# Constant matmuls in TensorE's waits, stores on two queues, and contiguous transposes in the tail of an attention and Fourier kernel

## The chip, the cores and the metric

The kernel runs on one core of a Trainium2 chip. The metric is device time in microseconds (us). Four timed executions of the kernel before took 3204.36 to 3206.36 us, with a median of 3204.9 us. One execution was recorded by the hardware profiler; the page and the trace that are quoted here come from it.

Engines are named as the profile names them: PE is TensorE's matrix multiply and PEld its weight load, DVE is VectorE, ACT is ScalarE, POOL is GpSimd, SP is SyncE (here only a queue that issues DMAs). L12 is line 12 of the kernel file. A 32-bit float (f32) matmul leaves two records in the trace, and so does its weight load.

## The reference

The input is x, 4 images of 64 channels and 96 x 96 pixels, in f32. Two layers follow each other, each of the form x + layer(group_norm(x)):

```python
# layer 0: attention over the 9216 pixels, with sigmoid weights
energy = jnp.einsum('bcn,bcm->bnm', Q, K)          # Q, K: 8 channels
out = jnp.einsum('bcm,bnm->bcn', V, jax.nn.sigmoid(energy)).reshape(B, C, H, W) + x
scale = jax.nn.sigmoid(mlp(out.mean((2, 3))) + mlp(out.max((2, 3))))
y = out * scale[:, :, None, None]

# layer 1: a spectral convolution
u_hat = jnp.fft.rfft2(u, norm='ortho')
top = jnp.einsum('bchw,cohw->bohw', u_hat[:, :, :16, :16], R_pos)
bot = jnp.einsum('bchw,cohw->bohw', u_hat[:, :, H - 16:, :16], R_neg)
# all other modes are zero
y = jnp.fft.irfft2(v_hat, s=(H, W), norm='ortho')
```

Group norm has 32 groups of two channels. Only 32 rows (the first 16 and the last 16) times 16 columns of the spectrum are used, so layer 1 is four small products with constant matrices (along w, along h, back along h, back along w) with one channel mixing per mode between them.

## The kernel before

The four images are handled as two pairs; a pair's 2 x 64 channels fill the 128 partitions. Attention of pair 0 and then of pair 1 takes the first 3106 us. Layer 1 of pair 0 is done in small steps beside the attention of pair 1 (class `Hidden`, lines 223 to 334). Layer 1 of pair 1 has nothing left to hide behind: it is the tail, written out in program order from line 577 on, and it is what the change edits.

The tail, by its parts:

- **Statistics and the transform along w** (lines 618 to 631). For each of 12 strips of 8 image rows, DVE forms layer 0's result (`combine`, L158) and transposes the strip in blocks of 32 x 32 (L623); ACT sums the squares (L624); PE multiplies the transposed strip with the matrix `fw` (L631) into a two-bank tile `pa`. Four strips fill one `pa`.
- **The transform along h** (lines 636 to 645). After each fourth strip (n = 0, 1, 2) DVE transposes `pa` into a tile `a` (L637), and four matmuls add its part to the two banks `pu` (L642). They read `a` in consecutive elements as the moving operand. These matmuls stand in PE's order where the scheduler puts them: those of n = 1 stand ahead of the last strips' L631.
- **Statistics' end** (L655 to L660). The variance, `group_stats`' second and third step (matmul L136, DVE L138, POOL L139), and `spread` (matmuls L169), which turns them into a scale per channel.
- **The spectrum `u`** (L667 to L677). DVE transposes `pu` (L670), and ACT and DVE scale it into `ut` (L672 to L675, and L183).
- **Mixing** (`mix`, L185 to L209, called from L687). For each q from 0 to 7 and two halves: 8 matmuls (L198), then a copy from PSUM to a tile `vm` (L112 on DVE, L114 on ACT, in turns). There are four `vm` tiles. After the second half, four stores of 64 KB each write `vm` to a DRAM tensor `vd`; all 32 stores are issued by SP (L209).
- **The way back through DRAM** (L210 to L221). The mixed modes are read back in another order into `vt`, in 64 KB loads: four after q = 3, issued by POOL, and four after q = 7, two by SP and two by ACT. The loads of the second group wait for all stores of q = 4 to 7.
- **Back along h** (L693 to L704). 16 matmuls (L700) into 8 PSUM banks `pz`. Their moving operand is `vt`, viewed as `"q (k o) -> q o k"`: 16 elements that lie 64 elements apart, 16 times.
- **The transposes to `z`** (L705 to L710). Eight DVE transposes L708 read a bank in order and write `z[:H, :, ...]` with a step of 128 elements between consecutive elements.
- **Back along w and the result** (L713 to L727). For each of 8 groups, 12 matmuls (L720) whose weights are `z[rows, h, :]`, 128 consecutive elements, and whose moving operand is the constant `gw`; DVE adds the residual (L722), and after each second group three stores of 384 KB go out on SP and ACT (L726).

The mixing weights are 32 rows of 512 KB. Those that aren't there yet are loaded by POOL during the tail (L650, L590), each as soon as the tile that it takes the place of is free.

PSUM pools: `ps_m` (two buffers of one tag) serves the small matmuls of the statistics, `ps_v` (8 buffers) the mixing.

Of the kernel before, what the change touches and what calls it, by code (L numbers as in the profile page):

```python
# [40 lines left out]
P = 128  # L41
# [36 lines left out]
def tile_kernel(ctx: ExitStack, tc: tile.TileContext, x, cst, late, spec, out):  # L78
# [37 lines left out]
    def group_stats(stats, bank, name):  # L116
# [17 lines left out]
        def third():  # L134
            pv = bank(f"pv_{name}")
            nc.tensor.matmul(pv[:, 0:1], pav, t, start=True, stop=True)  # L136
            ve = small.tile([P, 1], F32, tag="ve", name=f"ve_{name}")
            nc.vector.tensor_scalar(ve, pv[:, 0:1], GN_EPS, None, ALU.add)  # L138
            nc.gpsimd.tensor_tensor(mr[:, 1:2], ve, nhalf, ALU.pow)  # L139

# [5 lines left out]
    class Layer1:  # L146


        def __init__(self, p, gate, bank, move, load_queue):
            self.p, self.gate, self.bank, self.move = p, gate, bank, move  # L150
            self.load_queue = load_queue
# [9 lines left out]
        def spread(self, mr):  # L161
# [5 lines left out]
            for b in range(2):  # L167
                for part in range(2):
                    nc.tensor.matmul(pr[bass.ts(part, C), bass.ts(b, 2)],  # L169
                                     ident[:, bass.ts(b, C)], mr, start=True, stop=True)  # L170
# [14 lines left out]
        def mix(self, q, half):  # L185
# [8 lines left out]
            for k in range(2):  # L194
                kw = half * 2 + k
                for g in range(4):
                    at = ((4 * q + g) * KW + SIDE * kw) * 4
                    nc.tensor.matmul(  # L198
# [9 lines left out]
            for g in range(4):  # L208
                nc.sync.dma_start(self.vd[4 * q + g], self.vms[q][32 * g:32 * g + 4 * SIDE, :])  # L209
            if q % 4 == 3:  # L210
                if self.vt is None:
                    self.vt = self.place_of_vt()
                row, M = 4 * SIDE * KW * C, KW // SIDE * C
                for b in range(2):
                    for slot in range(2):
                        to = 64 * b + 32 * slot + 4 * q - 12
                        of = self.vd[4 * q - 12, 2 * slot + b, :]
                        of = bass.AP(tensor=of.tensor, offset=of.offset,
                                     ap=[[row, 16], [4 * KW * C + M, SIDE], [1, M]])
                        self.load_queue(q, slot).dma_start(  # L220
                            self.vt[to:to + 16, :].rearrange("h (n m) -> h n m", n=SIDE), of)  # L221

    class Hidden(Layer1):


        def __init__(self, p, gate, bank, move, work):
            super().__init__(p, gate, bank, move, lambda q, slot: nc.sync)
# [349 lines left out]
    with tc.tile_pool(name="tail", bufs=1, reuse_waits="tile") as tail, \  # L577
# [22 lines left out]
        for i in range(4):  # L600
            wts[NSLOT - 4 + i] = w_mid[:, bass.ts(i, KW * C)]
            nc.gpsimd.dma_start(wts[NSLOT - 4 + i], spec[NSLOT - 4 + i])

        small_bank = psum("ps_m")
        l1 = Layer1(1, gate, lambda name: small_bank.tile([P, NB], F32, tag="m", name=name, bufs=2),
                    evacuate, lambda q, slot: nc.gpsimd if q == 3 else (nc.sync, nc.scalar)[slot])
# [10 lines left out]
        pu = [pu_bank.tile([P, NB], F32, tag=f"u{b}", name=f"pu_{b}") for b in range(2)]  # L617
        for s in range(NSTRIP):
# [11 lines left out]
            for k in range(NSQ):  # L630
                nc.tensor.matmul(pa[:, bass.ts(i, STRIP // NSQ)], fw[:, bass.ts(k, P)], v[:, k],  # L631
                                 start=(k == 0), stop=(k == NSQ - 1))
            if i < NSTRIP // NSQ - 1:
# [3 lines left out]
            nc.vector.transpose(a.rearrange("q (k c) -> q c k", c=SQ),  # L637
                                pa.rearrange("q (h c) -> q c h", c=SQ))
            for part in range(2):
                for b in range(2):  # L640
                    rows = bass.ts(b, C)
                    nc.tensor.matmul(pu[b], fh[rows, part, bass.ts(n, P)],  # L642
                                     a[rows, bass.ts(part, NB)],
                                     start=(n == 0 and part == 0),
                                     stop=(n == NSQ - 1 and part == 1))
# [9 lines left out]
        var = small.tile([P, 1], F32, tag="var", name="var")  # L655
        nc.vector.tensor_reduce(var, squares, AX.X, ALU.add)
        nc.vector.tensor_scalar(mv[:, 1:2], var, 1.0 / N, None, ALU.mult)
        for step in steps[1:]:
            step()
        l1.spread(mr)  # L660

# [22 lines left out]
        mix_bank = psum("ps_v", 8)  # L684
        l1.bank = lambda name: mix_bank.tile([P, NB], F32, tag="v", name=name)
        l1.place_of_vt = lambda: place_of("w0", "vt")
        for q in range(KH // 4):  # L687
            l1.mix(q, 0)
            l1.mix(q, 1)

# [5 lines left out]
        for i in range(4):  # L696
            for e in range(2):
                for b in range(2):
                    rows = bass.ts(b, 2 * KH)
                    nc.tensor.matmul(  # L700
# [4 lines left out]
        z = tail.tile([P, SQ, P], F32, tag="z", name="z_1")  # L705
# [107 lines left out]
```

## Time and profile before

| What | us |
|---|---|
| median of 4 timed executions | 3204.9 |
| their range | 3204.36 to 3206.36 |
| the profiled execution's own time | 3206.36 |
| its span, first to last instruction | 3204.6 |
| attention of both pairs, to the last L426 | 3106.5 |
| the tail, 3106.5 to 3204.6 | 98.1 |

The mean granted TensorE clock is 0.991 of full speed over the span. In the tail it is not: it goes between 1.0 and 0.5, as the stretches quoted in the prediction list.

How to read what is quoted: in a list of stretches each line is a stretch of the span, its length, then for PE, PEld, DVE, ACT and POOL the busy time and in brackets the number of instructions touching the stretch, then the granted clock, the mean busy share of the DMA engines and the GB/s that they moved. In a list of groups each line is a line of the kernel, engine and operation, output <- inputs, shapes, the count, and after the bar the busy time in us and the mean duration of one in ns. In the chain, each line is the start, the length and the instruction that the end of the program was waiting for in that stretch. An answer on one line of the kernel gives the count, and after it the shortest, the median and the longest duration in ns.

### The profile page before, as it was taken

The page shows a single profiled execution, that of the slowest core. Times are in us where ns is not written, and L with a number is a line of the kernel's source. Part 1 is how long each engine was busy: PE and PEld are TensorE (multiplying, and loading weights), DVE is VectorE, ACT ScalarE, POOL GpSimd, SP SyncE. Part 2 cuts the span into 40 slices and gives each one's busy share as a digit, 9 for nine tenths or more (in the row PEclk, how much of TensorE's full clock was granted, in tenths as well). Part 3 has the DMA queues.
Part 4 walks back from the last instruction along what each step waited for, and adds up shares of the span by engine and source line. Part 5 has one row for each costly group of instructions (what it writes and reads, how often), then busy time and mean ns, then how long its engine had stood idle before and what let it go on. Part 6 is the DMA issues. An engine that isn't in the chain of part 4 may idle for free.

```text
span 3204.6 us, 39104 instructions
## 1 busy us (share of the span) xinstructions
PE 3147.3 (98%) x17464; PEld 1068.4 (33%) x17464; DVE 399.8 (12%) x838; ACT 2432.8 (76%) x1765; POOL 22.4 (1%) x45
## 2 busy tenths in 40 slices
PE   7999999999999999999999999999999999999996
PEld 3333333333333333334333333333333333333334
DVE  4200000000000000003331110000000110000025
ACT  3688888888888888886677777777777777888871
POOL 0000000000000000000000000000000001000001
PEclk9999999999999999999999999999999999999997
DMA  3000000000000000000130100221010112000025
GB/s 139 1 1 1 1 1 1 1 1 1 1 1 1 1 1 1 1 1 1 40 92 14 40 1 30 82 70 37 13 28 10 40 36 97 33 1 1 11 77 177
DMA packets 39032, 86.78 MB, mean 27 GB/s; under 512 B 10672, under 2 KB 17584, under 8 KB 38768
## 3 DMA queue, kind: packets, MB, share of 16 engines
q1 hardware_dynamic: 32240, 61.75, 6.5%
q0 software_dynamic: 4880, 17.63, 1.5%
q10 hardware_dynamic: 1744, 4.91, 0.4%
q8 instruction: 136, 2.23, 0.3%
q14 instruction: 32, 0.26, 0.0%
HBM read 62.77 MB, written 21.50 MB: 26 GB/s over the span
## 4 chain that ended last, share of the span: by engine, by line
PE 97%; DVE 1%; DMA 1%; SPq 0%; issue 0%; ACT 0%; POOL 0%; ACTq 0%
PE acc L426 74%; PE e L415 18%; PE pv L385 1%; PE pv L198 1%; PE py L330 1%; PE pk L376 1%; PE pq L396 1%; DMA x<-in_x_dram 0%; PE py L720 0%; PE pt L253 0%; PE pz L309 0%; PE pa L631 0%; PE pu L290 0%; DVE z L708 0%; SPq L209 0%; PE pu L642 0%
## 5 line engine op out<-in xcount | busy, mean ns | idle before, releaser
L419 ACT ACTIVATE at<-e 128x1536 f32<-128x1536 f32 x1728 | 2412.5, 1448 | 683.4 <-PE e L415 683.2
L426 PE MATMUL acc<-at,vT 128*64 128x512 f32 x10368 | 2418.9, 601 | 0.0
L426 PEld LDWEIGHTS acc<-at,vT 128*64 128x64 f32 x10368 | 668.3, 136 | 1294.5 <-issue 1279.1
L415 PE MATMUL e<-q,kT 32*128 32x512 f32 x5184 | 636.4, 461 | 1.3 <-ACT at L419 1.3
L415 PEld LDWEIGHTS e<-q,kT 32*128 32x128 f32 x5184 | 257.9, 183 | 642.2 <-issue 583.0
L356 DVE TENSOR_SCALAR full_q<-pq,cs 128x256 f32<-128x256 f32 x36 | 17.4, 484 | 1557.2 <-PE pq L396 1557.1
L569 DVE SCALAR_TENSOR_TENSOR x<-acc,x 128x512 f32<-128x512 f32 x36 | 24.9, 691 | 294.3 <-PE acc L426 294.3
L385 PE MATMUL pv<-cs,x 128*128 128x128 f32 x288 | 43.4, 295 | 0.1
L332 DVE TENSOR_TENSOR x<-py,x 128x384 f32<-128x384 f32 x24 | 13.4, 558 | 226.0 <-PE py L330 226.0
L406 DVE CAST q<-q 32x256 fp32r<-32x256 f32 x144 | 40.9, 284 | 3.8
L385 PEld LDWEIGHTS pv<-cs,x 128*128 128x128 f32 x288 | 36.2, 197 | 14.2 <-DVE full_k L356 12.9
L505 DVE COPY ws<-pv 128x512 f32<-128x512 f32 x16 | 11.1, 691 | 216.3 <-PE pv L198 216.3
L364 DVE SCALAR_TENSOR_TENSOR q<-high_q,cs,full_q 64x256 fp32r<-64x256 f32 x72 | 34.6, 480 | 2.4
L505 DVE COPY xT<-pt 96x512 f32<-96x512 f32 x24 | 16.4, 685 | 114.1 <-PE pt L253 114.1
L356 DVE TENSOR_SCALAR full_k<-pk,cs 128x256 f32<-128x256 f32 x36 | 17.4, 483 | 103.4 <-PE pk L376 103.4
L387 DVE TENSOR_TENSOR vT<-pv,cs 128x512 f32<-128x512 f32 x36 | 24.9, 691 | 8.8 <-PE pv L385 8.8
L571 DVE TENSOR_REDUCE maxs<-x 128x1 f32<-128x512 f32 x36 | 24.7, 685 | 1.1
L376 PE MATMUL pk<-x,cs 128*64 128x256 f32 x144 | 23.3, 395 | 1.5 <-DVE x L144 1.5
L433 DVE BATCH_NORM_STATS2 stats<-x 128x6 f32<-128x512 f32 x36 | 22.2, 677 | 8.1 <-DMA x<-in_x_dram 8.1
L396 PE MATMUL pq<-x,cs 128*64 128x256 f32 x144 | 22.1, 386 | 0.0
L330 PE MATMUL py<-cs,ws 128*128 128x384 f32 x48 | 21.9, 539 | 0.0
L128 PE MATMUL pm_l<-mv_l,cs 128*128 128x1 f32 x8 | 1.7, 286 | 20.5 <-DVE mv_l L124 19.8
(96 smaller groups left out, 448.6 us busy)
## 6 DMA issues: line engine op xcount, KB each, us to landing
ws<-in_spec_dram SPq DMA_DIRECT2D x32, 512.0 KB
x<-in_x_dram SPq DMA_DIRECT2D x15, 512.0 KB
out_dram<-x SPq DMA_DIRECT2D x18, 384.0 KB
w<-in_spec_dram POOLq DMA_DIRECT2D x10, 512.0 KB, 6.6
old<-in_x_dram SPq DMA_DIRECT2D x12, 384.0 KB
x1d<-x SPq DMA_DIRECT2D x12, 384.0 KB
x<-x1d SPq DMA_DIRECT2D x12, 384.0 KB
w_early<-in_spec_dram POOLq DMA_DIRECT2D x9, 512.0 KB, 9.4
```

Source lines behind the costliest of these rows:

```text
L198: nc.tensor.matmul(pv[bass.ts(g, 32), :].rearrange("q (n k o) -> q n k o", n=SIDE, o=C)[:, :, k, :], self.ut[:, at:at + 32], self.wts[4 * ...
L330: nc.tensor.matmul(py[:, :4 * W], self.z[:, i, :], named("gw"), start=True, stop=True)
L356: nc.vector.tensor_scalar(u, src, bias, None, ALU.add)
L364: mark[0] = nc.vector.scalar_tensor_tensor(dst, h.bitcast(F32), is_low, u, ALU.mult, ALU.add)
L376: nc.tensor.matmul(pp[cols, :NB // 2], named("wk")[:, cols], src[:, e, :, :], start=True, stop=True)
L385: nc.tensor.matmul(pp[:, bass.ts(i, P)], xs[p][:, bass.ts(4 * s + i, P)], named("wv"), start=True, stop=True)
L396: nc.tensor.matmul(pq[rows, :half], named("wq")[:, rows], xs[p][:, n * NB + e * half:n * NB + (e + 1) * half], start=True, stop=True)
L406: nc.vector.tensor_copy(q[to:to + 32, cols], q[of:of + 32, cols])
L415: nc.tensor.matmul(eb[i // PART][:, i % PART, :], kT[r:r + 32, t // 4, :], q[r:r + 32, :], start=True, stop=True)
L419: nc.scalar.activation(at[:, bass.ts(h, PART), :], eb[h], AF.Sigmoid)
L426: nc.tensor.matmul(acc[half, :], vT[:, j, half], at[:, i, :], start=(j == 0), stop=(j == NCH - 1))
L505: l1 = Hidden(0, gate, bank_a, lambda dst, src: nc.vector.tensor_copy(dst, src), work)
```

## The change

The change has four parts.

1. **Constant matmuls.** A new function `occupy(n, behind, pool)` issues n matmuls of the constant tile `cs` by itself (128 x 128 weights, 512 columns, f32) into a PSUM tile that nothing reads, behind a given PE instruction. It is called three times: 4 matmuls after `spread`, 7 after the mixing, and 1 after back along h. The PSUM pools make room: `ps_m` has one buffer and the idle tile, `ps_v` 7 buffers and the idle tile.
2. **Mixing's stores on two queues.** Of the four stores of each q, two are issued by SP and two by POOL. The read-back is issued after q = 5 (rows of q = 0 to 3, on SP and POOL) and after q = 7 (on SP and ACT).
3. **Transposes with contiguous outputs.** L637 and L708 write consecutive elements. Their readers then read with steps: the matmuls along h read `a` with a step of 32 elements as the moving operand, and the matmuls back along w load their weights from `z` with a step of 32 elements.
4. **Order along h.** The matmuls of n = 1 are put behind the last L631, and those of n = 2 behind the matmul of the variance (L136); the variance's steps come ahead of `spread` and the late weight loads in the program.

In the scheduled program PE's order becomes: all L631, then along h of n = 1, L136, along h of n = 2, L169, 4 constant matmuls, mixing, 7 constant matmuls, back along h, 1 constant matmul, back along w. DVE's order is unchanged.

```diff
@@ Layer1.mix
             for g in range(4):
-                nc.sync.dma_start(self.vd[4 * q + g], self.vms[q][32 * g:32 * g + 4 * SIDE, :])
-            if q % 4 == 3:
+                self.queues[g % 2].dma_start(self.vd[4 * q + g],
+                                             self.vms[q][32 * g:32 * g + 4 * SIDE, :])
+
+            if q in (5, 7):
...
+                first = KH // 2 * (q == 7)
                 for b in range(2):
                     for slot in range(2):
-                        to = 64 * b + 32 * slot + 4 * q - 12
-                        of = self.vd[4 * q - 12, 2 * slot + b, :]
+                        to = 64 * b + 32 * slot + first
+                        of = self.vd[first, 2 * slot + b, :]
...
-                        self.load_queue(q, slot).dma_start(
+                        self.queues[slot if q == 5 else 2 * slot].dma_start(
@@ the tail
+        def occupy(n, behind, pool):
+
+
+            pd = pool.tile([P, NB], F32, tag="idle", name=f"idle_{behind.ins.name}")
+            with tc.issue_after(behind.ins):
+                for _ in range(n):
+                    nc.tensor.matmul(pd, cs[:, :P], cs[:, :NB], start=True, stop=True)
+
         small_bank = psum("ps_m")
-        l1 = Layer1(1, gate, lambda name: small_bank.tile([P, NB], F32, tag="m", name=name, bufs=2),
-                    evacuate, lambda q, slot: nc.gpsimd if q == 3 else (nc.sync, nc.scalar)[slot])
+        l1 = Layer1(1, gate, lambda name: small_bank.tile([P, NB], F32, tag="m", name=name),
+                    evacuate, (nc.sync, nc.gpsimd, nc.scalar))
...
             a = place_of(f"a{n}", f"a_{n}")
-            nc.vector.transpose(a.rearrange("q (k c) -> q c k", c=SQ),
-                                pa.rearrange("q (h c) -> q c h", c=SQ))
-            for part in range(2):
-                for b in range(2):
-                    rows = bass.ts(b, C)
-                    nc.tensor.matmul(pu[b], fh[rows, part, bass.ts(n, P)],
-                                     a[rows, bass.ts(part, NB)],
-                                     start=(n == 0 and part == 0),
-                                     stop=(n == NSQ - 1 and part == 1))
+            nc.vector.transpose(a, pa.rearrange("q (h c) -> q c h", c=SQ))
+            along_h.append(lambda n=n, v=a.rearrange("q (c s k) -> q s k c", s=2, k=KW): [
+                nc.tensor.matmul(pu[b], fh[bass.ts(b, C), part, bass.ts(n, P)],
+                                 v[bass.ts(b, C), part], start=(n == 0 and part == 0),
+                                 stop=(n == NSQ - 1 and part == 1))
+                for part in range(2) for b in range(2)])
+            if n == 0:
+                along_h[0]()
+
+        with tc.issue_after(last.ins):
+            along_h[1]()
...
+        steps[1]()
+        with tc.issue_after(steps[2]().ins):
+            along_h[2]()
...
         l1.spread(mr)
+        occupy(4, l1.last, small_bank)
...
-        mix_bank = psum("ps_v", 8)
-        l1.bank = lambda name: mix_bank.tile([P, NB], F32, tag="v", name=name)
+        mix_bank = psum("ps_v", 1)
+        l1.bank = lambda name: mix_bank.tile([P, NB], F32, tag="v", name=name, bufs=7)
...
+        occupy(7, l1.last, mix_bank)
...
-        z = tail.tile([P, SQ, P], F32, tag="z", name="z_1")
+        z = tail.tile([P, P, SQ], F32, tag="z", name="z_1")
         for i in range(4):
             for b in range(2):
-                nc.vector.transpose(
-                    z[:H, :, b * C + i * NO:b * C + (i + 1) * NO].rearrange("q h o -> q o h"),
-                    pz[b][i][:H, :])
+                nc.vector.transpose(z[:H, b * C + i * NO:b * C + (i + 1) * NO, :], pz[b][i][:H, :])
         banks.close()
         py_bank = psum("ps_y", 2)
+        occupy(1, last, py_bank)
...
-                    nc.tensor.matmul(py[:, j, bass.ts(i, W)], z[rows, HG * g + i, :],
+                    nc.tensor.matmul(py[:, j, bass.ts(i, W)], z[rows, :, HG * g + i],
```

## The prediction

> **What bounds the kernel now.** I read the list of stretches first, cut at the tail's steps. Attention fills the span to 3106.5 and isn't touched, so only the last 98 us can move.
>
> ```profile
> 3121.50:3142.40 20.90, 16.45 (x74) 10.48 (x74) 15.94 (x21) 5.97 (x12) 6.45 (x12) 1.00 0.79 272
> 3142.40:3147.18 4.78, 0.32 (x9) 0.27 (x10) 4.37 (x12) 2.09 (x2) 0.66 (x2) 0.82 0.68 243
> 3147.18:3152.29 5.11, 5.11 (x49) 2.69 (x53) 0.69 (x1) 0.58 (x1) 0.45 (x1) 0.50 0.30 103
> 3152.29:3163.70 11.41, 11.40 (x212) 6.90 (x204) 4.84 (x7) 3.51 (x6) 0.57 (x2) 1.00 0.64 113
> 3163.70:3174.23 10.53, 0.00 (x1) 0.03 (x1) 0.00 (x0) 0.58 (x1) 1.49 (x3) 0.61 0.59 130
> 3174.23:3179.60 5.37, 5.37 (x24) 4.77 (x26) 3.33 (x4) 0.00 (x0) 0.00 (x0) 0.50 0.00 0
> 3179.60:3183.45 3.85, 2.55 (x12) 1.08 (x9) 3.79 (x5) 0.00 (x0) 0.00 (x0) 0.94 0.00 0
> 3183.45:3199.10 15.65, 14.24 (x192) 13.98 (x192) 10.86 (x8) 0.00 (x0) 0.00 (x0) 0.50 0.56 219
> ```
>
> PE idles 4.5 us ahead of the mixing and 10.5 us behind it; the granted clock falls to 0.5 in both gaps, and the first 5.11 us of mixing run at half clock. The last two steps are mostly at half clock too.
>
> Then the chain of waits, for what ends last in each step:
>
> ```profile
> 3133.21 1.99 PE pu L642 x8
> 3135.20 3.23 PE pa L631 x14
> ...
> 3138.45 1.89 DVE a L637
> ...
> 3140.40 2.04 PE pu L642 x8
> ...
> 3168.53 2.14 DMA vd<-vm
> ...
> 3170.92 3.06 DMA vt<-vd
> ...
> 3176.26 7.14 DVE z L708 x8
> ```
>
> Along h, n = 1's matmuls stand ahead of the last strips, which then stand ahead of the last transpose. Behind the mixing the chain runs through SP: the last copy to `vm` ends at 3164.38, but SP issues its last store at 3168.53, since 32 stores at about 0.46 us each are queued on it.
>
> Third, one operation at two clocks: L631 at 0.5 (first line) and 1.0 (second), L700 at 0.5 (third) and 1.0 (fourth).
>
> ```profile
> L631 PE MATMUL pa<-xt,lc x6: 630/632/632, 3115.5 to 3117.6; 128*128 128x256 f32 x6
> ...
> L631 PE MATMUL pa<-xt,lc x14: 378/380/451, 3118.0 to 3120.9; 128*128 128x256 f32 x14
> ...
> L700 PE MATMUL pz<-vt,cs x17: 604/607/611, 3175.6 to 3179.1; 64*96 64x256 f32 x17
> ...
> L700 PE MATMUL pz<-vt,cs x10: 605/606/608, 3179.4 to 3181.5; 64*96 64x256 f32 x10
> ```
>
> L631 reads consecutive elements and drops from 632 to 380 ns with the full clock. L700 reads elements 256 bytes apart and stays at 606; by the records' starts one follows the other in 0.43 us at both clocks (L631: 0.43, then 0.216). So a moving operand read with a step goes at the half-clock pace whatever the clock. This is the row that the change has to be measured by, since it gives steps of 128 bytes to two more readers.
>
> Last, the groups of the two kinds of transpose, and the weight load that gets a step:
>
> ```profile
> L720 PEld LDWEIGHTS py<-cs,z 32*128 32x128 f32 x192 | 14.0, 323 | 2.2 <-DVE z L708 2.2
> ...
> L708 DVE STREAM_TRANSPOSE z<-pz 96x512 f32<-96x512 f32 x8 | 7.1, 1043 | 12.6 <-PE pz L700 12.6
> ...
> L670 DVE STREAM_TRANSPOSE t<-pu 128x512 f32<-128x512 f32 x2 | 1.3, 694 | 2.1 <-PE pu L642 2.1
> ```
>
> A transpose of 512 elements takes 1043 ns with a stepped output, 694 with a contiguous one. Back along w is PE's weight loads: 192, three side by side, 64 x 0.2225 = 14.2 us.
>
> **Part 1, along h.** L642 has 4 matmuls per n, two beside each other: 8 records, 4 pairs of 512 columns at 0.43 us, 1.99 us in all. With the step, at the L700 pace, a pair is 2 x 0.433 = 0.866 us, and n takes 4 x 0.866 + 0.16 = 3.6 us. The transpose L637 loses its stepped output but keeps a stepped input, which no row prices alone: it gains between 0 and 0.66 us (the difference to L670's 0.65 us per 512, twice, against 1.89); I take 0.3. Now in order. n = 0 starts at 3123.5 - 0.3 and leaves PE at 3126.7. Then 20 L631 matmuls follow, 2 x 0.216 each, 8.6 us: 3135.4, and the last strip (DVE, done at 3134.97, now 3134.4) puts that at 3135.7. n = 1 follows to 3139.2, L136 takes 0.2, and n = 2 (its transpose done by 3137.6, hidden) runs 3139.4 to 3143.0. Before it ended at 3142.4: **+0.6**. Without a price for the step n = 2 would start when its transpose ends, some 1.9 to 3.3 us earlier than before; so the ends are -3.3 and +0.8, and I take the row nearest in kind, L700. What is queued on POOL behind these: the loads of the weight rows that take `a1` and `a2`, needed only at q = 7, over 15 us later.
>
> **Part 2, the mixing's clock.** Four constant matmuls, 2 x 0.43 us each, fill PE from the end of L169 (now 3143.3) to 3146.8; `u` is ready 4.8 us behind n = 2 as before, at 3147.8. So PE waits 1 us instead of 4.5, and the fill isn't on the path. The granted clock changes at multiples of 3.41 us in this trace (3145.46, 3152.29, 3165.94, 3179.60, 3183.01); it fell after stretches of that length in which PE was busy for 0.67 or 1.16 us, and held after one with 1.65. A wait of 1 us shouldn't drop it. Worth: the same matmuls at twice the clock, half of 5.11, **-2.55**; the ends are 0 (it drops all the same) and -2.55.
>
> On this the Trainium skill, "TensorE: Matmul & The Clock Gate", section "What's actually happening", says that about 3.4 us of sustained work restores the clock. Here it took 5.11 us. By the page the fill would be worth 1.7 us and the sum below -4.5; the trace decides.
>
> **Part 3, the stores.** Each q now has two stores on SP (0.46 us each) and two on POOL (0.53, as its L220 loads), against 1.74 us per q of mixing (copies at full clock, one per 0.87 us), so neither queue falls behind. From the last copy: POOL's second store starts 0.65 us later and lands 2.3 us behind that (SP's took 2.14; POOL's loads of this size 2.8, SP's 2.7). Then, as now, 3.55 us from the last landing to L700 (3170.69 to 3174.23). In all 6.5 us instead of 9.85: **-3.3**. Ends: -3.8 (POOL as quick as SP) and +1.0 (POOL's store takes the 6.6 us of its 512 KB loads). What waits behind new waits: SP's read-back after q = 5 waits for the POOL stores of q = 3, which land about 0.9 us before SP gets there, and q = 6 and 7's stores stand behind it; the copy of q = 4 needs q = 0's `vm`, landed 2 us before. Fewer PSUM buffers (7 for 8, 1 for 2) cost nothing: copies follow the matmuls within one half. The 7 constant matmuls take 6.0 us of a 7.2 us gap.
>
> **Part 4, back along h.** L700 keeps its pace, 7.9 us from start to end, clock or not; so the full clock brings nothing here. The transposes were just as fast as PE (busy 7.13 us); at 0.65 us each they now follow PE, and the last ends 8.6 us behind L700's start instead of 9.17: -0.5. The one constant matmul fits before it at full clock (0.86 us), and delays L720 by 0.8 us at half clock; I give it +0.2. **-0.3**, ends -0.5 and +0.3.
>
> **Part 5, back along w.** The weights get a 128-byte step. At L700's pace per column (0.433 us for 256) 128 columns take 0.217 us, against 0.214 now at half clock: 64 x 0.003, **+0.15**. Low end: no price for the step and a full clock; then DVE's 1.36 us per group and the 340 GB/s of the output stores bound the rest, -2. High end: the step doubles the load, 64 x 0.214 = +13.7.
>
> The Trainium skill, "SBUF — State Buffer", section "Door 1: The DMA port swizzle", says that steps beyond 16 bytes cost full bandwidth. No run here shows a 128-byte step; by the page parts 1 and 5 stand, by L700's row (256 bytes) alone part 1 could also be -2.6 and the sum -8.6.
>
> **Sum.** +0.6 - 2.55 - 3.3 - 0.3 + 0.15 = -5.4 us. Made on the profiled execution (span 3204.6, own time 3206.36): 3201.0. That one was the slowest of four, 1.46 above the median, so the median becomes 3204.9 - 5.4 = **3199.5**. 0.2% is 6.4 us, about what a measurement of this kernel can tell from no change; I predict a gain within that.
>
> **Rivals.**
> - *The 128-byte step is free for L642.* Against it: L700. For it: its step is half as long. n = 2 then ends 2.6 us early instead of 0.6 late: 3204.9 - 8.6 = 3196.3, and with free weight loads as well 3194.
> - *POOL's stores land late.* For it: its 512 KB loads take 6.6 us; against: its 64 KB loads 2.8. Part 3 shrinks to about -0.5: 3202.3.
> - *The fills don't hold the clock.* For it: stepped reads may count as little work: PE showed 2.55 us busy of 3.41 on L700 before 3183.01, and the clock fell. Mixing starts at half clock, perhaps the fill runs over: 3204.9 - 2.8 = 3202.1.
> - *Slower: stepped weight loads cost more than the moving operand's pace.* L720's chain is only weight loads. From 0.31 us a load the gain is gone, from 0.41 the kernel is slower by 0.2%; at 0.43 it is 3204.9 - 5.4 + 13.7 = 3213. Against it: at half clock a load already takes as long per column as L700's stepped read.
>
> **How the numbers follow.** Forecast 0.60, free step 0.17, POOL late 0.08, clock not held 0.08, slower 0.07. The forecast spreads by some 1.5 us (the four executions lie 2 us apart), so a quarter of it is beyond 6.4 us. Faster: 0.15 + 0.17 = 0.32. Slower 0.07. The rest, 0.61, within. The range takes in all but the slower rival and the tails: 3193.8 (both steps free, 3194.3, less 0.5 of spread) to 3204.0 (POOL late, 3202.3, and 1.7 of spread).
>
> **What would show it.** L642 at about 1.03 us a record (0.866 + 0.16) instead of 0.59; the clock 1.0 from the start of the mixing, which takes 13.9 us instead of 16.5; L700 starting 6.5 us behind the last `vm` copy; L700 still at 606 ns; L708 at 0.69 us; L720's loads still 14 us. It would be wrong if L642 stays at 0.59, if L720's loads change, or if the clock falls ahead of the mixing.

## The result, and the profile after

The changed kernel has a median of 3200.4 us (39 executions, 3199.28 to 3202.29) against 3205.5 us for the kernel before, measured beside it (59 executions, 3203.1 to 3207.52). The ratio is 0.9985, with a 95% interval of 0.9981 to 0.999: 5.1 us faster, 0.16%, so inside the 0.2% band that the forecast named, and still clear of no change. Forecast was 3199.5 us.

The profiled execution of the changed kernel took 3200.08 us, with a span of 3198.3 us, 6.3 us less than the one before. Of this, 1.7 us lies ahead of the change: attention ends at 3104.8 us instead of 3106.5. In the twelve experiments below, whose attention is the same code, it ends anywhere from 3104.2 to 3106.4 us, so this is scatter. The tail went from 98.1 to 93.5 us, and only that is compared from here on.

The list of stretches of the kernel after, cut at its steps as before: wait for `u`, mixing, way back through DRAM, back along h in three pieces, back along w in two. The columns are those explained in front of the prediction.

```profile
3141.31:3146.10 4.79, 3.91 (x17) 1.66 (x18) 4.38 (x12) 2.12 (x2) 0.65 (x2) 1.00 0.50 178
3146.10:3160.80 14.70, 14.70 (x258) 10.42 (x259) 5.54 (x8) 4.68 (x8) 7.91 (x17) 1.00 0.73 154
3160.80:3168.50 7.70, 5.52 (x13) 2.13 (x12) 0.00 (x0) 0.00 (x1) 1.27 (x3) 1.00 0.56 121
3168.50:3171.06 2.56, 2.56 (x12) 1.77 (x14) 0.60 (x1) 0.00 (x0) 0.00 (x0) 1.00 0.00 0
3171.06:3174.47 3.41, 3.41 (x19) 2.91 (x17) 2.56 (x5) 0.00 (x0) 0.00 (x0) 0.50 0.00 0
3174.47:3177.02 2.55, 2.52 (x10) 0.77 (x6) 2.07 (x4) 0.00 (x0) 0.00 (x0) 1.00 0.00 0
3177.02:3181.30 4.28, 4.28 (x60) 4.28 (x60) 1.84 (x2) 0.00 (x0) 0.00 (x0) 1.00 0.02 4
3181.30:3192.86 11.56, 10.15 (x138) 9.90 (x135) 9.02 (x7) 0.00 (x0) 0.00 (x0) 0.50 0.76 295
```

The first line shows PE busy for 3.91 of the 4.79 us in which `u` is made (it was 0.32 of 4.78), and the clock at 1.0 there and through the whole mixing. The third line shows 7.70 us from the last copy to back along h. In the fourth to sixth lines the clock falls and rises within back along h, though PE shows no idle time.

The chain of waits of the kernel after:

```profile
3121.09 3.69 PE pu L652 x8
3124.78 8.93 PE pa L644 x40
3133.71 3.62 PE pu L652 x8
...
3137.64 3.67 PE pu L652 x8
...
3161.61 3.26 DMA vd<-vm
...
3165.35 3.11 DMA vt<-vd
...
3168.50 7.43 PE pz L718 x32
3175.93 1.05 PE idle_I-15694_15708 L614 x2
...
3177.02 14.46 PE py L737 x184
```

Along h (L642, now L652) PE is on the chain without a break from 3121.09 on: the transposes no longer count. SP's row of issues, 7.4 us of the chain before (3161.08 to 3168.47), is down to 1.4 us (3160.17 to 3161.57); behind it stands a store that takes 3.26 us to land, where it took 2.14. Back along h is PE's until 3175.93 (the transposes of 7.14 us are gone from the chain). Behind it the chain names the constant matmul (L614), but the last transpose ends at the same time, 3176.96 against 3176.98, just before back along w starts.

Answers on single lines of the kernel after: along h, back along h at full and at half clock, the weight loads back along w at full and at half clock, and the two transposes.

```profile
L652 PE MATMUL pu<-a,lc x24: 1032/1032/1107, 3121.1 to 3140.2; 64*128 64x512 f32 x24
...
L718 PE MATMUL pz<-vt,cs x12: 605/607/620, 3168.5 to 3171.0; 64*96 64x256 f32 x12
...
L718 PE MATMUL pz<-vt,cs x17: 605/607/609, 3170.7 to 3174.1; 64*96 64x256 f32 x17
...
L737 PEld LDWEIGHTS py<-cs,z x57: 290/307/311, 3177.2 to 3181.2; 32*128 32x128 f32 x57
...
L737 PEld LDWEIGHTS py<-cs,z x117: 286/308/311, 3181.3 to 3189.8; 32*128 32x128 f32 x117
...
L650 DVE STREAM_TRANSPOSE a<-pa x3: 1199/1236/1250, 3119.8 to 3133.7; 128x1024 f32<-128x1024 f32 x3
...
L726 DVE STREAM_TRANSPOSE z<-pz x8: 668/690/712, 3170.5 to 3176.3; 96x512 f32<-96x512 f32 x8
```

What reads with a step has one duration at both clocks: 607 ns for 256 columns, 307 ns for a weight load. L652 takes 1032 ns with a step of 128 bytes; before, with consecutive elements, its records took 590:

```profile
L642 PE MATMUL pu<-a,lc x24: 588/590/694, 3123.5 to 3141.8; 64*128 64x512 f32 x24
```

Both kinds of transposes are a third shorter.

The tail by its steps, each cut at the same events in both traces (us):

| step | before | after | difference | forecast |
|---|---|---|---|---|
| end of attention to the end of along h | 35.89 | 36.47 | +0.58 | +0.6 |
| to the first mixing matmul | 4.79 | 4.84 | +0.05 | 0 |
| mixing, to the last copy's end | 17.21 | 14.71 | -2.50 | -2.55 |
| to the first matmul back along h | 9.84 | 7.70 | -2.14 | -3.3 |
| to the first matmul back along w | 9.22 | 8.52 | -0.70 | -0.3 |
| to the end of the span | 21.14 | 21.29 | +0.15 | +0.15 |
| tail | 98.09 | 93.52 | -4.57 | -5.4 |

### The profile page after: what moved, and what is told of

Read it like the earlier page. It is cut to its first block, busy times and chain, and to the rows that moved or that the text cites. A ratio compares the mean times of both kernels' runs of the same rounds, so it can differ in the third digit from the quotient of the medians.

```text
span 3198.3 us, 39167 instructions
## 1 busy us (share of the span) xinstructions
PE 3158.0 (99%) x17488; PEld 1071.8 (34%) x17488; DVE 396.2 (12%) x838; ACT 2432.8 (76%) x1765; POOL 29.1 (1%) x59
## 4 chain that ended last, share of the span: by engine, by line
PE 98%; DVE 1%; DMA 1%; issue 0%; ACT 0%; SPq 0%; POOL 0%; ACTq 0%; DVEq 0%
PE acc L430 74%; PE e L419 18%; PE pv L389 1%; PE pv L199 1%; PE py L334 1%; PE pq L400 1%; PE pk L380 1%; PE py L737 0%; DMA x<-in_x_dram 0%; PE pt L257 0%; PE pu L652 0%; PE pa L644 0%; PE pz L313 0%; PE pu L294 0%; PE pz L718 0%; PE pa L267 0%
```

## The experiments

All experiments start from the changed kernel; their short diffs are against it. Times are medians, ratios are to the kernel before as it ran beside them (3205.1 us for the first four, 3205.0 for the next four, 3205.5 for the last four). With intervals about 0.2% wide, the times of two experiments often can't be told apart; the lengths of the steps in their traces can, and the readings go by these.

### Each part taken back

**Without the four constant matmuls ahead of the mixing.**

```diff
         l1.spread(mr)
-        occupy(4, l1.last, small_bank)
```

> The changed kernel without the 4 constant matmuls ahead of the mixing. My theory: PE then waits about 4.8 us for the spectrum, the granted clock falls to 0.5 in that wait as it did before, and the first 3.4 to 6.8 us of mixing run at half clock: first L199 matmul to last copy 16 to 18 us instead of 14.7, the kernel 1.7 to 3 us slower than the changed one (ratio to before about 0.9992). Rival, the clock holds without them because the stepped reads of L652 keep PE busy longer: no difference, 14.7 us.

Measured: 3203.37 us, ratio 0.9994 (0.9985 to 1.0003). The stretches of this run, from the wait for `u` to the end of the mixing:

```profile
3142.56:3147.29 4.73, 0.28 (x8) 0.22 (x9) 4.35 (x12) 2.08 (x2) 0.61 (x2) 0.77 0.52 186
3147.29:3151.93 4.64, 4.64 (x44) 2.51 (x48) 0.69 (x1) 0.59 (x1) 0.51 (x2) 0.50 0.34 113
3151.93:3164.27 12.34, 12.34 (x218) 7.55 (x211) 4.85 (x7) 4.10 (x7) 7.48 (x16) 1.00 0.78 141
```

PE idles again, and the first 4.64 us of mixing run at half clock. Mixing takes 16.98 us instead of 14.71, and no other step moves by over 0.15 us. The four matmuls are worth 2.3 us here, half of those 4.64 us, as a clock of half should cost. The rival that the fills don't hold the clock is refuted for this place.

**All stores on one queue.**

```diff
-                self.queues[g % 2].dma_start(self.vd[4 * q + g],
-                                             self.vms[q][32 * g:32 * g + 4 * SIDE, :])
+                nc.sync.dma_start(self.vd[4 * q + g], self.vms[q][32 * g:32 * g + 4 * SIDE, :])
-            if q in (5, 7):
+            if q in (3, 7):
...
-                        self.queues[slot if q == 5 else 2 * slot].dma_start(
+                        self.queues[1 if q == 3 else 2 * slot].dma_start(
```

> The changed kernel with all 32 stores on SP and the first read-back after q = 3 on POOL, as before. My theory: SP's issue is the limit again, last copy to the first L718 matmul back from 7.7 to about 9.9 us, and since the mixing is now faster than SP (0.87 us per half against 0.93 us for two stores) rather more: 10 to 12 us; the kernel 2 to 4 us slower than the changed one. Rival, the landing of the stores is the limit and not their issue: at most 0.5 us slower.

Measured: 3203.65 us, ratio 0.9994 (0.9985 to 1.0004). From the last copy to back along h it takes 10.81 us, 3.1 more than with two queues and 1.0 more than in the kernel before. Mixing is still 14.71 us. So on one queue the faster mixing gains only 27.05 - 25.52 = 1.5 us for mixing and way back together: SP can't issue 32 stores any faster, and what the clock saves goes partly into a longer backlog on SP. The two parts were costed as independent terms, and they aren't: without the second queue the fill would have been worth 1.5, not 2.5.

Its chain shows how fast the last store lands from one queue:

```profile
3165.67 2.15 DMA vd<-vm
...
3168.07 3.12 DMA vt<-vd
```

**Step back in the write of `a` (along h).**

```diff
-            nc.vector.transpose(a, pa.rearrange("q (h c) -> q c h", c=SQ))
-            along_h.append(lambda n=n, v=a.rearrange("q (c s k) -> q s k c", s=2, k=KW): [
+            nc.vector.transpose(a.rearrange("q (k c) -> q c k", c=SQ),
+                                pa.rearrange("q (h c) -> q c h", c=SQ))
+            along_h.append(lambda n=n, v=a.rearrange("q (s m) -> q s m", s=2): [
```

> The changed kernel with the old form of the transposes along h: the transpose writes with a step, the matmuls read consecutive elements; the new order is kept. My theory (the step in the moving read is what costs): L652's records back from 1032 to 590 ns, 3.69 to 1.99 us per n, the transposes from 1.23 back to 1.89 us; the last L652 ends about 34.1 us behind the end of attention instead of 36.5; the kernel about 2.4 us faster than the changed one. Rival, the transposes are what bounds this stage: no gain, or up to 2 us slower (3 x 0.66).

Measured: 3199.18 us, ratio 0.9981 (0.9972 to 0.9991). The answers on the matmuls along h and on the transpose:

```profile
L653 PE MATMUL pu<-a,lc x24: 589/589/693, 3123.1 to 3139.8; 64*128 64x512 f32 x24
...
L650 DVE STREAM_TRANSPOSE a<-pa x3: 1921/1943/1971, 3121.1 to 3136.3; 128x1024 f32<-128x1024 f32 x3
```

Along h ends at 34.31 us instead of 36.47. The contiguous transposes of `a`, taken alone, cost 2.2 us: they save 0.7 us each on DVE and add 1.7 us to each group of four matmuls on PE. This run has the old layout in the new order along h, so its 34.31 us against 35.89 before also give the worth of the order (part 4 of the change, which no run takes back alone): about 1.6 us.

**Step back in the write of `z`.**

```diff
-        z = tail.tile([P, P, SQ], F32, tag="z", name="z_1")
+        z = tail.tile([P, SQ, P], F32, tag="z", name="z_1")
...
-                nc.vector.transpose(z[:H, b * C + i * NO:b * C + (i + 1) * NO, :], pz[b][i][:H, :])
+                nc.vector.transpose(
+                    z[:H, :, b * C + i * NO:b * C + (i + 1) * NO].rearrange("q h o -> q o h"),
+                    pz[b][i][:H, :])
...
-                    nc.tensor.matmul(py[:, j, bass.ts(i, W)], z[rows, :, HG * g + i],
+                    nc.tensor.matmul(py[:, j, bass.ts(i, W)], z[rows, HG * g + i, :],
```

> The changed kernel with the old form of z: L726's transposes write with a step of 128 elements, L737's weights are consecutive. My theory: the transposes take 1.04 us again and end about 0.5 us later; L737's loads go at 0.213 us at half clock and near 0.11 us at full clock, so back along w gains only as long as the clock is 1.0, at most 2 us; between 1.5 us faster and 0.5 us slower than the changed kernel. Rival, contiguous outputs are a clear gain here: 1.5 us or more slower than the changed kernel.

Measured: 3199.5 us, ratio 0.9982 (0.9972 to 0.9991). Back along h takes 0.6 us longer (transposes of 1007 ns), back along w and the output 1.4 us less. Two stretches of back along w show why, the first two groups and the others:

```profile
3177.18:3179.75 2.57, 2.03 (x48) 1.87 (x48) 1.37 (x2) 0.00 (x0) 0.00 (x0) 1.00 0.02 6
3181.05:3191.50 10.45, 9.03 (x124) 8.78 (x120) 8.15 (x6) 0.00 (x0) 0.00 (x0) 0.50 0.84 325
```

At full clock 48 consecutive loads take 1.87 us of PEld; in the changed kernel the same 48, with their step, take 3.44:

```profile
3177.02:3180.46 3.44, 3.44 (x48) 3.44 (x48) 1.36 (x1) 0.00 (x0) 0.00 (x0) 1.00 0.02 5
```

After that the clock is at 0.5, and the step makes next to no difference (8.78 us for 120 records here and 9.90 for 135 in the changed kernel are 73 ns a record in both). In all, the contiguous transposes of `z` cost 0.8 us in these traces. The step of the weights thus has the price that the slower rival gave it (nearly twice), but only against a full clock, and the kernel before never had one there.

**Without the constant matmuls behind the mixing and behind back along h.**

```diff
-        occupy(7, l1.last, mix_bank)
...
-        occupy(1, last, py_bank)
```

> The changed kernel without the 7 constant matmuls behind the mixing and the one behind back along h. My theory: L718 goes at 606 ns whatever the clock and L737's loads at 0.217 us whatever the clock, so these fills buy next to nothing: back along h 7.4 to 7.9 us, the kernel 0 to 0.6 us slower than the changed one. Rival, they hold the clock and make both steps faster: 2 us or more slower without them.

Measured: 3201.44 us, ratio 0.9989 (0.998 to 0.9998); that is 1.0 us above the changed kernel, more than the 0 to 0.6 expected. The answer on back along h, and its stretch:

```profile
L717 PE MATMUL pz<-vt,cs x32: 605/607/712, 3168.4 to 3175.4; 64*96 64x256 f32 x32
```

```profile
3168.38:3176.98 8.60, 7.64 (x33) 4.39 (x33) 5.24 (x8) 0.00 (x0) 0.00 (x0) 0.63 0.00 0
```

Over this step the clock is at 0.63 instead of 0.80, and the matmuls take the same 607 ns. The step lasts 8.60 us (8.52 with the fill). These eight matmuls buy nothing in back along h, since its matmuls read with a step. In the trace of this run the end came 1.2 us later all the same, which is the size of the difference of the medians: the last output store is issued at 3193.27 us, as in the changed kernel (3193.29), and the span ends 6.2 us behind it instead of 5.0. The DMA engines show how, here in the last stretch of the stores, first in this run and then in the changed kernel:

```profile
3197.05:3198.20 1.15, 0.00 (x0) 0.00 (x0) 0.00 (x0) 0.00 (x0) 0.00 (x0) 0.50 0.06 24
3195.90:3197.00 1.10, 0.00 (x0) 0.00 (x0) 0.00 (x0) 0.00 (x0) 0.00 (x0) 0.50 0.75 291
```

A share of 0.06 is one engine of 16: one engine still had 1.2 us of stores to move when the others were done. During the output the trace also holds one 16 KB load of the instruction queue. By the DMA packets it lasts 1.89 us in this run and 1.52 us in the other run without these fills, and 0.92 to 1.12 us in the eleven traces of the changed kernel and the experiments that have them. That this load holds up the engine which ends last fits, but no run isolates it, nor why it comes at a worse time without the fills.

### The step put into PSUM

The three places where a step costs PE something are reads. A fourth place for it is the write of the matmul's result into PSUM: the columns are taken in the order in which they lie, and the output is addressed with the step.

**Along h, the step in the write to `pu`.**

```diff
-            along_h.append(lambda n=n, v=a.rearrange("q (c s k) -> q s k c", s=2, k=KW): [
-                nc.tensor.matmul(pu[b], fh[bass.ts(b, C), part, bass.ts(n, P)],
+            along_h.append(lambda n=n, v=a.rearrange("q (c s k) -> q s c k", s=2, k=KW): [
+                nc.tensor.matmul(pu[b].rearrange("q (k c) -> q c k", c=SQ), fh[bass.ts(b, C), part, bass.ts(n, P)],
```

> The changed kernel with the same contiguous transposes along h, but the matmuls go through the columns in the order of a, so that they read runs of 16 consecutive elements and write PSUM with a step of 32 elements instead. If only the moving read's step costs: L652's records 590 ns, the last of them ends 32.5 to 33.5 us behind the end of attention instead of 36.5, the kernel 3 to 4 us faster than the changed one. If a step in the PSUM write costs as much: 1032 ns and no difference.

Measured: 3197.01 us, ratio 0.9975 (0.9965 to 0.9984).

```profile
L652 PE MATMUL pu<-a,lc x24: 589/589/693, 3120.7 to 3136.9; 64*128 64x512 f32 x24
...
L650 DVE STREAM_TRANSPOSE a<-pa x3: 1201/1239/1250, 3119.4 to 3133.3; 128x1024 f32<-128x1024 f32 x3
```

Both are at their contiguous pace: 589 ns for the matmul and 1239 ns for the transpose. Along h ends at 33.08 us, 3.4 less than in the changed kernel, and 1.2 less than with the step in the transpose's write. What now comes last ahead of the final groups is DVE's own work on the strips.

**Back along h, the step in the write to `pz`.**

```diff
-                        pz[b][i][:H, :].rearrange("q (o e k) -> q e o k", e=2, k=KW)[:, e],
+                        pz[b][i][:H, :].rearrange("q (o e k) -> q e k o", e=2, k=KW)[:, e],
...
-                        l1.vt[rows, :].rearrange("q (k o) -> q o k", o=C)[:, bass.ts(i, NO), :],
+                        l1.vt[rows, :].rearrange("q (k o) -> q k o", o=C)[:, :, bass.ts(i, NO)],
```

> The changed kernel with back along h going through its columns in the order of vt: it reads runs of 16 consecutive elements and writes PSUM with a step of 32. If only the moving read's step costs, and the clock is 1.0: L718's records fall from 606 to about 380 ns, PE needs 4 us instead of 7.4, the transposes (8 x 0.65 us) are the bound, and L737 starts about 6.4 us behind L718 instead of 8.5: 2 us faster than the changed kernel. If the PSUM write's step costs as much, or the clock is 0.5: no difference.

Measured: 3198.29 us, ratio 0.998 (0.9971 to 0.9989).

```profile
L718 PE MATMUL pz<-vt,cs x32: 376/376/425, 3169.9 to 3173.9; 64*96 64x256 f32 x32
...
L726 DVE STREAM_TRANSPOSE z<-pz x8: 669/670/712, 3171.1 to 3175.3; 96x512 f32<-96x512 f32 x8
```

The matmul takes 376 ns instead of 607, and back along h 6.10 us instead of 8.52. Here the clock stays at 1.0 from the first matmul to the last. It is the read's step and not the clock that cost the time: the stepped matmuls took 607 ns at both clocks.

### Where the stores' gain went

**The first read-back one q earlier.**

```diff
-            if q in (5, 7):
+            if q in (4, 7):
...
-                        self.queues[slot if q == 5 else 2 * slot].dma_start(
+                        self.queues[slot if q == 4 else 2 * slot].dma_start(
```

> The changed kernel with the first read-back issued after q = 4 instead of q = 5. My theory for the one term that came out smaller than forecast (last copy to L718 7.7 us, not 6.5): the last stores stand behind the first read-back's loads in the DMA queues and so land 3.1 to 3.3 us after issue instead of 2.1. Then they land after 2.1 to 2.5 us here, and the kernel is about 1 us faster than the changed one. Rival, stores issued by two queues at once, or by POOL, simply take 3.2 us: no difference.

Measured: 3200.56 us, ratio 0.9987 (0.9977 to 0.9997). The way back takes 7.30 us instead of 7.70, but the landing that it was meant to shorten did not get shorter:

```profile
3162.90 3.33 DMA vd<-vm
```

In the other runs with two queues this step takes 7.4 to 7.9 us with its DMAs as in the changed kernel, so 0.4 us is the size of its scatter; the landing itself takes 2.8 to 3.4 us in these traces. My theory, that the first read-back delays the last stores, falls. What the traces do show is the mean busy share of the DMA engines (last but one column) from the time at which the last four stores are issued, in the changed kernel:

```profile
3160.80:3161.60 0.80, 0.80 (x3) 0.35 (x2) 0.00 (x0) 0.00 (x1) 0.80 (x3) 1.00 1.05 204
3161.60:3162.60 1.00, 1.00 (x4) 0.41 (x3) 0.00 (x0) 0.00 (x0) 0.47 (x1) 1.00 0.95 195
3162.60:3163.60 1.00, 1.00 (x4) 0.39 (x3) 0.00 (x0) 0.00 (x0) 0.00 (x0) 1.00 1.01 246
```

and with one queue, before and while its last store lands:

```profile
3164.00:3165.00 1.00, 1.00 (x4) 0.41 (x3) 0.00 (x0) 0.00 (x0) 0.00 (x0) 1.00 0.79 201
3165.00:3166.00 1.00, 1.00 (x3) 0.19 (x1) 0.00 (x0) 0.00 (x0) 0.00 (x0) 1.00 0.76 148
3166.00:3167.00 1.00, 0.15 (x1) 0.00 (x0) 0.00 (x0) 0.00 (x0) 0.00 (x0) 1.00 0.76 127
```

Two queues put four stores of 64 KB out within about a microsecond; the engines are then full for 2.8 us, while one queue, with a store every 0.46 us, leaves a quarter of them idle. That the fuller engines make each landing longer fits these rows, but no run isolates it; a second queue other than POOL was not tried either.

### Versions that might beat both

**Both steps in PSUM.** The edits of the two runs above together.

> The changed kernel with both matmuls along h (L652 forwards, L718 back) reading in order and writing PSUM with a step. Both single changes moved only their own step (3.4 and 2.4 us), so I expect their sum: the stretch behind the end of attention 93.5 - 3.4 - 2.4 = 87.7 us, the median near 3194.6 us, ratio to before about 0.9967. A rival: what one gives is taken back by the DMA-bound output at the end or by the clock falling earlier, and the sum is 4 us or less.

Measured: 3194.64 us, ratio 0.9965 (0.9953 to 0.9978). Along h ends at 33.08 us and back along h takes 6.06 us, as in the two runs alone; the sum of the two gains by the medians is 3.4 + 2.1 = 5.5, and 5.8 was measured.

**The same, without the constant matmuls behind the mixing and behind back along h.**

```diff
-        occupy(7, l1.last, mix_bank)
...
-        occupy(1, last, py_bank)
```

> The version with both in PSUM, without the 7 constant matmuls behind the mixing and the one behind back along h. In the changed kernel these bought nothing that its steps could use. Now L718 can use the full clock: I expect its records at 590 to 620 ns (half clock) instead of 376, back along h 8 to 9 us instead of 6.1, and the kernel 2 to 2.5 us slower than with them. Rival: the transposes are the bound there and hide it: at most 0.5 us.

Measured: 3196.71 us, ratio 0.9972 (0.996 to 0.9984), 2.1 us more than with them. Back along h takes 8.00 us instead of 6.06, at 631 ns a matmul instead of 376. The same fill that bought nothing ahead of stepped reads is worth 1.9 us ahead of reads in order. The output's end was 1.2 us later here too, so that the tails of the two traces differ by 3.4 us; the medians differ by less.

**The weights of back along w with a smaller step.** `z` is laid out so that s image columns lie side by side, which leaves the weights a step of 4s bytes. With s = 4 (16 bytes) and s = 2 (8 bytes):

```diff
-        z = tail.tile([P, P, SQ], F32, tag="z", name="z_1")
+        z = tail.tile([P, SQ // 2, P, 2], F32, tag="z", name="z_1")
...
-                nc.vector.transpose(z[:H, b * C + i * NO:b * C + (i + 1) * NO, :], pz[b][i][:H, :])
+                nc.vector.transpose(
+                    z[:H, :, b * C + i * NO:b * C + (i + 1) * NO, :].rearrange("q x o h -> q o x h"),
+                    pz[b][i][:H, :].rearrange("q (o x h) -> q o x h", o=NO, h=2))
...
-                    nc.tensor.matmul(py[:, j, bass.ts(i, W)], z[rows, :, HG * g + i],
+                    nc.tensor.matmul(py[:, j, bass.ts(i, W)], z[rows, (HG * g + i) // 2, :, (HG * g + i) % 2],
```

> As the version with both in PSUM, and z laid out so that the weights of L737 lie 4 elements (16 bytes) apart and the transposes write runs of 4 elements. If a step of 16 bytes is free: the loads go at 0.21 us at half clock and 0.11 us at full clock, back along w is up to 1.5 us shorter while the clock holds. If any step costs: 0.217 us at both clocks and no gain. The transposes: 0.69 us if runs of 4 are as good as contiguous, 1.0 us if not, which would cost up to 2 us.

> As the version with both in PSUM, with the weights of L737 2 elements (8 bytes) apart and the transposes writing runs of 2. If a step of 8 bytes is free for a weight load and one of 16 is not: loads 0.11 us at full clock here and 0.217 there. The transposes between 0.69 and 1.0 us. Kernel between 1.5 us faster and 2 us slower than the version with both in PSUM.

Measured: 3195.34 us, ratio 0.9968 (0.9955 to 0.998) with 16 bytes; 3193.29 us, ratio 0.9961 (0.9949 to 0.9974) with 8 bytes. The stretches at full clock at the start of back along w, first with 128 bytes (both steps in PSUM), then 16, then 8 (busy times of PE and PEld alone):

```profile
3170.97:3174.34 3.37, 3.37 (x48) 3.37 (x48) 1.00 0.02 5
```

```profile
3172.22:3175.00 2.78, 2.78 (x36) 2.78 (x36) 1.00 0.02 6
```

```profile
3170.35:3172.30 1.95, 1.95 (x48) 1.95 (x48) 1.00 0.03 8
```

The stretch over its count gives the pace of a weight load's record (a load has two): 70 ns with 128 bytes, 77 with 16 and 41 with 8 (39 with consecutive weights, from the run with the step in the write of `z`). The small step of 8 bytes costs the transposes nothing either (670 ns). At half clock the paces are 73, 77 and 71 ns, and the clock falls 2.9 to 4.0 us into the step in all of them, so the full rate helps only two of the eight groups. Back along w and the output take 21.20, 22.29 and 20.29 us: 16 bytes are a loss, 8 bytes a gain. With 8 bytes the tail is 86.5 us long, and the kernel beats the changed one and the one before: 12.2 us below the latter.

## Why the prediction was right

The forecast of 3199.5 us, 5.4 below the median shown of before, stands against 3200.4, which is 5.1 below the kernel before as it ran beside it, and the kind of result, a gain of under 0.2%, was the one given the most chance. The stated range, 3193.8 to 3204.0, took in every rival but the slower one, so being inside it says little; the parts say more. Part 1 to Part 5 are the five terms of the prediction's sum, not the four parts of the change:

- **Part 1** was right in size and for its reason. A pair of stepped matmuls was put at 0.866 us and a group at 3.6; the trace has 1032 ns a record and 3.62 to 3.69 us a group, and the step ended 0.58 us later. Taking the stepped read at L700's pace, from a row with twice the step, decided the sign here. The transposes' saving was taken as 0.3 us within ends of 0 to 0.66; it is the whole 0.66. The first of the three lets along h start earlier by as much (16.30 us behind the end of attention instead of 17.00); the other two are hidden, because PE ends last from there on. The groups, at 3.62 to 3.69 us where the forecast's schedule gave them 3.5 to 3.6, and L136, at 0.31 us instead of 0.2, took this back, so that +0.58 meets +0.6 partly by chance. The rival of a free 128-byte step is refuted by the same record.
- **Part 2** was right: clock at 1.0 from the first mixing matmul, -2.50 us. The run without the fill shows the cause. By an estimate from the Trainium skill's 3.4 us until the clock is restored ("TensorE: Matmul & The Clock Gate", section "What's actually happening") it would have been 1.7 us; that run spent 4.64 us at half clock, so the trace's 5.11 was the better guide. What the forecast didn't say is that this gain leans on Part 3; on one queue it is 1.5 us.
- **Part 3** is the term that was mis-sized: -3.3 us forecast, -2.1 measured. The queues emptied as described, but the forecast let the last store land 2.3 us behind its issue, from SP's 2.14 us with one queue, and it took 3.26 (2.8 to 3.4 in all traces with two queues). The rows ahead of the forecast that were nearer were those of loads of the same size: POOL's 2.8 us, and the 3.06 us of the last load in its own chain. The rival of late POOL stores (-0.5) had a right kind of reason, a slower landing, at more than twice its size, and not on POOL alone: the store that ends the chain of the changed kernel is SP's own.
- **Part 4** came out at -0.70 us against -0.3. L718 kept its 607 ns at both clocks, and the transposes became 0.69 us, as forecast; the 32 records took 7.43 us instead of the 7.9 that were carried over from L700. In the runs with the same layouts back along h, PE takes 7.4 to 8.0 us and the step 8.5 to 9.0, and the forecast step (8.9) lies within; so most of the miss is scatter that one trace doesn't show. The constant matmul's +0.2 us for half clock wasn't due: the clock was 1.0 there (sixth line of the first list), and the last transpose ended at the same time.
- **Part 5** was right, +0.15 us. The run with consecutive weights shows that it was right by cover: the slow clock hides the step's price. The slower rival, 0.43 us for three load records side by side at half clock, is refuted: 3.44 us for 48 at full clock and 9.90 us for 135 at half clock are 0.22 us for three, at both clocks.

The errors of Part 3 and Part 4 partly cancel by chance, +1.2 and -0.4; 0.8 us remain. The trace before also happened to have a late end of attention, so that the two spans differ by 6.3 us while the tails differ by 4.6. The medians differ by 5.1; where the other 0.5 us lie, one trace of each kernel doesn't show.

Left open: why four stores from two queues land later (argued from the engines' busy share alone); why one DMA engine ended 1.2 us later in both traces without the last fills; and what lets the clock fall during back along w, where it did so in the changed kernel and in every experiment, with consecutive weights too, and in eight of these traces after 3.41 us in which PE shows no idle time.

## What to carry to other kernels

When a layout change moves a step from a write to a read, find the reader and its engine in the trace before counting the writer's gain: here a third off the transposes cost 2.2 us along h and a net 0.8 us behind the mixing. A reader that already has a step, as back along h had before the change, is locked at half-clock pace, and warming the clock buys nothing for it. A third place is worth a try first, the matmul's own write into PSUM, which took the step for nothing in both stages; in back along h it made the fills worth 1.9 us that had been worth nothing there. And parts that meet on a queue don't add: cost the faster producer together with the queue that drains it.

## What the runs showed of the hardware that was not expected

- A matmul's write to PSUM with a step of 32 elements cost nothing: 589 ns for 512 columns with the step in the output, 589 with none; 376 ns for 256 columns, against 607 with the step in the read. The Trainium skill, "SBUF — State Buffer", section "Door 1: The DMA port swizzle", says that any non-contiguous PSUM access slows matmuls significantly. These runs don't show it for writes with this step.
- A transpose that reads PSUM with a step and writes consecutive elements has its full rate: 1.23 us for 1024 elements, about twice the 0.65 us for 512. Its write with a step costs half as much again (1.94 us).
- For f32 weight loads the price of a step sets in between 8 and 16 bytes: at full clock the pace is 41 ns with 8 and 77 with 16, the latter no better than the 70 with 128 bytes. The same section of the skill gives SBUF lines of 16 bytes that want at least two accesses each for full bandwidth, which these numbers fit, and four f32 as the free step, which the 77 ns contradict.
- Matmuls with stepped reads also seem to count for less with the clock, as one rival supposed. In every trace the changes of the clock lie multiples of 3.41 us apart, as in the prediction's list. In the changed kernel, the last 3.41 us ahead of the fall within back along h held 2.56 us of stepped matmuls and nothing else, and in three experiments 1.9 to 2.1 us. About as much of the same matmuls, read in order, held the clock at 1.0 in the two runs with a smaller step of the weights. Such a stretch, of the run with the step in the write of `z`, with the one behind it, and then the same of the run with 8 bytes:

```profile
3166.78:3170.19 3.41, 2.13 (x10) 1.33 (x12) 0.17 (x1) 0.00 (x0) 0.00 (x0) 1.00 0.03 4
3170.19:3173.60 3.41, 3.41 (x18) 2.60 (x16) 3.41 (x5) 0.00 (x0) 0.00 (x0) 0.50 0.00 0
...
3163.02:3166.43 3.41, 2.14 (x19) 2.13 (x21) 1.02 (x2) 0.00 (x0) 0.00 (x0) 1.00 0.02 2
3166.43:3169.85 3.42, 2.85 (x19) 1.60 (x15) 3.42 (x7) 0.00 (x0) 0.00 (x0) 1.00 0.00 0
```

With the same busy time of PE, 10 stepped records went through in the first and 19 in order in the third. Stepped matmuls did hold the clock where they filled 3.2 us of the 3.41, in the run with the first read-back one q earlier. No run was made to separate this, and what the clock counts is not shown.
